# Image statistics of three images: ScalarE sums and squares in place of VectorE's statistics instructions

## The chip, the core and the metric

The kernel runs on one core of a Trainium2 chip. The engines of that core that matter here are TensorE (PE in the profile), VectorE (DVE), ScalarE (ACT), GpSimd (POOL, which issues the gathers) and SyncE (SP, which issues most other DMAs). Each engine works through its own queue in order; what one engine needs from another it waits for at a semaphore. The metric is the device time of one execution in microseconds. It was 2958.33 us before the change, the median of 10 runs (2955.92 to 2961.35).

## The reference

The input is x, four images of 256 channels by 64 x 64 pixels. Cut to what matters, the reference is:

```
x = x + deformable_conv(group_norm(x))     # 3x3, offsets and mask from a 3x3 conv
t = tokens(x)
t = t + attention(layer_norm(t))           # tied over rows, 4 x 4 maps per head
t = t + moe(layer_norm(t))                 # 8 experts, top 2
out = images(t)

group_norm(v): 32 groups of 8 channels; m, s = mean and variance over (8, 64, 64)
               (v - m) / sqrt(s + 1e-5)
```

The change is in the mean and the variance of the group norm. The kernel first makes the mean and the variance of every channel over its 4096 pixels. A small matmul with a block matrix of 1/8 then averages over the 8 channels of a group.

## The kernel before

The convolution comes first. An image is kept as two chunks of 128 channels (ch 0 and 1), 4096 pixels each, in a tile xraw. Its normalised form is turned to pixel rows and stored as a table in device memory. The convolution of an image then takes 288 steps: 32 rows of 128 pixels by 9 taps. The loop of line 1006 runs over the 4 x 288 steps of all images. One step n puts these into the queues, in this order:

- ScalarE: corner0(n + 4), line 808, the first of the four bilinear corners: gathered row times weight into a tile s. It needs the gather of step n + 4.
- VectorE: corners(n + 2), line 817, three multiply-adds (partial, s of the step before, s). The partial needs corner0(n + 2).
- TensorE: turned(n), line 831, two transposes of s into one of three tps tiles.
- ScalarE: to_sbuf(n - 1), line 839, copies a tps tile to sT.
- TensorE: product(n - 5), line 851, one matmul of 128 x 512 into acc.
- whatever else is due at this step, from the list todo.
- POOL: again(n + 1), line 798, the gather of step n + 11 into the buffer that corners has just left. There are ten gather buffers.

The order of VectorE, ScalarE, TensorE and GpSimd in this loop is the order in which it is written (line 997). Everything else for the next image is cut into small pieces that `pieces(b)` (line 438) lays down with a step each, counted from the start of the image that is being convolved. For images 1 to 3 these are: the four loads of 1 MB at steps 8, 18, 28, 38 (LOADS); the statistics of a quarter chunk, one block of 512 pixels a step, from seven steps after each load, so at steps 15 to 18, 25 to 28, 35 to 38 and 45 to 48; then the group means, the deviations and the reciprocal root (a power on GpSimd, line 482); then eight blocks of 512 pixels, 25 steps apart, each normalised on ScalarE (xs, line 549), turned, stored to the table and used for the offsets (po, line 583; oc, line 595; pt, line 604; om, line 615). The offsets become positions and weights on VectorE (lines 650 to 710). The first image makes its own statistics before the loop starts. Four of its own blocks (OWN, line 55) run inside its first steps, from steps 0, 19, 38 and 205.

The group of small PSUM tiles pm, po and pt comes from the pool ps_om, which has two buffers. Behind each block of 36 steps VectorE adds the residual (line 862, at steps 3 and 5 of the following block, so at steps 39 and 41 of an image for its first block), TensorE turns the sum back and ScalarE copies four tiles of it out (line 886, at steps 46, 48, 50, 52 for the first block).

The attention and the experts follow the convolution and are not touched.

The statistics are two lines:

```
V.bn_stats(st[:, ch, j, :], xr[:, ch, j * BLK : (j + 1) * BLK])
if j == NBLK - 1: V.bn_aggr(mv[:, ch, :], ...)
```

Of the kernel before, what the change touches and what calls it, by code (L numbers as in the profile page):

```python
# [9 lines left out]
F32 = mybir.dt.float32  # L10
I32 = mybir.dt.int32
AF = mybir.ActivationFunctionType
ALU = mybir.AluOpType
AX = mybir.AxisListType
# [3 lines left out]
P = 128  # L18
B, C, H, W = 4, 256, 64, 64
HW = H * W  # L20
NCH = C // P
# [16 lines left out]
BLK = 512  # L38
# [19 lines left out]
NBLK = HW // BLK  # L58
# [46 lines left out]
def conv_attn_moe_kernel(  # L105
# [23 lines left out]
    V, S, T, G = nc.vector, nc.scalar, nc.tensor, nc.gpsimd  # L129
# [205 lines left out]
    with ExitStack() as actx:  # L335
        aw = actx.enter_context(tc.tile_pool(name="a_w", bufs=1))
        ag = actx.enter_context(tc.tile_pool(name="a_gather", bufs=1))
        asm = actx.enter_context(tc.tile_pool(name="a_sm", bufs=5))
# [14 lines left out]
        ps_om = actx.enter_context(tc.tile_pool(name="ps_om", bufs=2, space=PSUM))  # L353
# [84 lines left out]
        def pieces(b):  # L438
# [3 lines left out]
            xr = xraw[b]  # L442
            st = asm.tile([P, NCH, NBLK, V.BN_STATS_DIM], F32, name=f"gst{b}", tag="gst", bufs=1)
            mv = asm.tile([P, NCH, V.BN_AGGR_DIM], F32, name=f"gmv{b}", tag="gmv", bufs=2)
# [4 lines left out]
            rs = asm.tile([P, NCH], F32, name=f"rs{b}", tag="grs", bufs=2)  # L449
            pm = []  # L450

            def stats(ch, j):
                V.bn_stats(st[:, ch, j, :], xr[:, ch, j * BLK : (j + 1) * BLK])
                if j == NBLK - 1:
                    V.bn_aggr(mv[:, ch, :], st[:, ch].rearrange("p j s -> p (j s)"))

            def group_of(src):
                pm.append(ps_om.tile([P, NCH], F32, name=f"pm{b}_{len(pm)}", tag="om"))
                T.matmul(pm[-1], group_mean, src, start=True, stop=True)
# [10 lines left out]
            n = FIRST  # L470
            out_ = later if b else first
            for ch in range(NCH):
                for j in range(NBLK):
                    at = LOADS[2 * ch + 2 * j // NBLK] + LANDED + j % (NBLK // 2)
                    out_.append((at if b else n, lambda ch=ch, j=j: stats(ch, j)))
                    n += 1
            out_.append((n + 1, lambda: group_of(mv[:, :, 0])))
            out_.append((n + 2, deviations))
            out_.append((n + 3, lambda: group_of(dv)))
# [262 lines left out]
            for q in range(NBLK + 1):  # L742
                at = n + 10 * q
# [7 lines left out]
            for q in range(EARLY):  # L751
                at = n + 20 * q
# [21 lines left out]
        ss, tps, sTs, accs, sums, backs, outs, last_corner, gathers = ({} for _ in range(9))  # L774
# [219 lines left out]
        for when, fn in pieces(0):  # L994
            todo.setdefault(when, []).append(fn)
        order = {nc.vector.engine, nc.scalar.engine, nc.tensor.engine, nc.gpsimd.engine}
        with tc.manual_schedule(engines=order):
# [8 lines left out]
            for n in range(total + TAP + OUT + 3 * NT):  # L1006
                b, at = divmod(n, STEPS)
                if at == LOADS[0] and b + 1 < B:
                    image_tile(b + 1)
                    for i, when in enumerate(LOADS):  # L1010
                        put_off(b * STEPS + when, lambda b=b, i=i: load_later(b, i))
                    for when, fn in pieces(b + 1):
                        put_off(b * STEPS + when, fn)
                if n < total and n % (NT * K2) == 0:
                    ended(n // (NT * K2))
                if n + LEAD < total:
                    corner0(n + LEAD)
                if n + 1 < total:
                    corners(n + 2)
                if n < total:  # L1020
                    turned(n)
                if LAG <= n < total + LAG:
                    to_sbuf(n - LAG)
                if 0 <= n - TAP < total:
                    product(n - TAP)
                if n == (B - 1) * STEPS + EARLIEST:
                    first_blocks()
                for fn in todo.pop(n, ()):
                    fn()

                if n + 1 + NGB < total:
                    again(n + 1)
# [10 lines left out]
    for b in range(B):  # L1043
        for j in range(NBLK):
            if j < HB:
                n = j * B + b
# [251 lines left out]
    with ExitStack() as bctx:  # L1298
# [266 lines left out]
        chores, sums = [], []  # L1565
# [623 lines left out]
```

## Time and profile before

| what | value |
|---|---|
| median of 10 runs | 2958.33 us (2955.92 to 2961.35) |
| the profiled execution | 2956.37 us, span 2954.7 us |
| busy in the span: PE, DVE, ACT, POOL | 95%, 83%, 64%, 60% |
| statistics, line 453 | 64 instructions, median 684 ns, first at 6.0 us, last at 1000.2 us |
| corners, line 817 | 3 x 1152 instructions, first at 66.5 us, last at 1760 us |
| corner0, line 808 | 1152 instructions, 509 ns each |
| mean granted TensorE clock | 0.992 |

The span runs from the first to the last instruction of one profiled execution. Busy times count an engine's instructions, not its waits. A row of a timeline gives the start, the duration, the engine, the line, the operation and the tiles as out<-in; in brackets stands the idle time before it and what ended it. The duration of a row is longer than its pitch, the time to the start of the next row on the same engine, because an instruction's end overlaps with the next one's start. The pitch is what an instruction costs a full queue.

### The profile page before, as it was taken

How to read it: one execution, taken by the hardware profiler on the slowest of the kernel's cores; microseconds unless marked ns; L12 is line 12 of the kernel's file. 1: busy time of each engine (PE TensorE's matmuls, PEld its weight loads, DVE VectorE, ACT ScalarE, POOL GpSimd, SP SyncE). 2: the span in 40 equal slices, each digit the busy share in tenths (PEclk: the TensorE clock that was granted, in tenths of full speed). 3: DMA queues.
4: the chain of work that ended last, by engine and by line, in shares of the span. 5: the costliest groups of instructions: out<-in, count | busy, mean ns of one | idle time of the engine just before them, and what ended most of it. 6: DMA issues, size and time to landing. Idle time of an engine off the chain costs nothing. (4 is left out here: it accounts for less than half of the span.)

```text
span 2954.7 us, 46107 instructions
## 1 busy us (share of the span) xinstructions
PE 2806.5 (95%) x11358; PEld 1651.6 (56%) x11358; DVE 2460.7 (83%) x6417; ACT 1890.7 (64%) x4459; POOL 1769.7 (60%) x1810
## 2 busy tenths in 40 slices
PE   5899999899998899998999999999999999999997
PEld 3455554455554455543444444445555688888885
DVE  5999989999999999999999987987778685446776
ACT  2666666566765566665766655765875666666675
POOL 2566666666666666667676753321767677774442
PEclk9999999999999999999999999999999999999998
DMA  8999999999999999999999978952565556657988
GB/s 290 368 357 409 406 366 405 405 395 399 406 410 408 380 403 406 403 387 399 399 396 374 387 289 154 170 89 79 184 195 181 176 176 192 205 147 254 339 279 278
DMA packets 347246, 911.97 MB, mean 309 GB/s; under 512 B 42301, under 2 KB 124516, under 8 KB 344679
## 3 DMA queue, kind: packets, MB, share of 16 engines
q0 software_dynamic: 208368, 689.10, 62.7%
q1 hardware_dynamic: 128183, 196.86, 21.4%
q10 hardware_dynamic: 10432, 23.07, 2.0%
q8 instruction: 95, 1.56, 0.2%
q14 instruction: 168, 1.38, 0.1%
HBM read 741.09 MB, written 170.54 MB: 309 GB/s over the span
## 5 line engine op out<-in xcount | busy, mean ns | idle before, releaser
L784 POOL DMA_INDIRECT g<-table,idx x1152 | 1122.0, 974 | 593.4 <-DVE s L817 491.7
L851 PE MATMUL acc<-sT,wconv_sb 128*128 128x512 f32 x2304 | 1183.0, 596 | 18.1 <-ACT sT L839 16.4
L808 ACT ACTIVATE s<-g,wts 128x256 f32<-128x256 f32 x1152 | 586.6, 509 | 327.6 <-DMA g<-table,idx 224.7
L817 DVE SCALAR_TENSOR_TENSOR partial<-g,wts,s 128x256 f32<-128x256 f32 x1152 | 565.0, 490 | 97.1 <-ACT s L808 18.2
L831 PEld LDWEIGHTS tps<-ident,s 128*128 128x128 f32 x2304 | 295.4, 147 | 624.7 <-issue 253.6
L817 DVE SCALAR_TENSOR_TENSOR s<-g,wts,s 128x256 f32<-128x256 f32 x1152 | 550.5, 478 | 0.0
L817 DVE SCALAR_TENSOR_TENSOR s<-g,wts,partial 128x256 f32<-128x256 f32 x1152 | 545.7, 474 | 0.5
L839 ACT COPY sT<-tps 128x256 f32<-128x256 f32 x1152 | 415.6, 361 | 165.0 <-PE acc L851 104.0
L831 PE MATMUL tps<-ident,s 128*128 128x128 f32 x2304 | 456.6, 280 | 61.1 <-DVE s L817 28.8
L1971 POOL DMA_INDIRECT ys_rows<-y,to x277 | 275.9, 996 | 223.0 <-DVE y L1966 166.0
L851 PEld LDWEIGHTS acc<-sT,wconv_sb 128*128 128x128 f32 x2304 | 348.4, 191 | 28.7 <-ACT sT L839 26.1
L1544 POOL DMA_INDIRECT xs_rows<-u,slots x256 | 253.2, 989 | 94.9 <-issue 68.9
L1943 PE MATMUL ph<-xT,w 128*128 128x256 f32 (+1 forms) x1288 | 270.1, 353 | 7.1 <-ACT hT L1947 4.1
L1961 PE MATMUL py<-w,hT 128*128 128x256 f32 x1108 | 266.4, 380 | 0.6 <-ACT w L1910 0.6
L1966 DVE TENSOR_TENSOR y<-py,w 128x512 f32<-128x512 f32 (+1 forms) x161 | 99.3, 617 | 188.9 <-ACT w L1904 81.5
L1943 PEld LDWEIGHTS ph<-xT,w 128*128 128x128 f32 x1288 | 211.9, 191 | 28.3 <-ACT hT L1947 6.1
L1961 PEld LDWEIGHTS py<-w,hT 128*128 128x128 f32 x1108 | 207.2, 190 | 27.4 <-ACT w L1910 1.0
L1947 ACT ACTIVATE hT<-ph,w 128x256 f32<-128x256 f32 (+1 forms) x322 | 136.2, 442 | 130.1 <-PE ph L1943 128.7
L324 DVE SCALAR_TENSOR_TENSOR junk<-q,k 128x512 f32<-128x512 f32 x224 | 141.3, 685 | 19.0 <-ACT k L1143 18.9
L583 PE MATMUL po<-xs,woff_sb 128*96 128x512 f32 x288 | 147.1, 592 | 0.0
L1326 DVE SCALAR_TENSOR_TENSOR mix<-pv,att,mix 128x512 f32<-128x512 f32 x192 | 132.7, 742 | 6.8 <-PE pv L1062 2.8
L1910 ACT COPY w<-early_state 128x768 f32 x161 | 132.8, 825 | 0.0
(294 smaller groups left out, 3436.1 us busy)
## 6 DMA issues: line engine op xcount, KB each, us to landing
xt<-xs_rows SPq DMA_DIRECT2D x116, 260.0 KB
yk<-ys_rows SPq DMA_DIRECT2D x56, 512.0 KB
table<-zt SPq DMA_DIRECT2D x96, 256.0 KB
g<-table,idx POOLq DMA_INDIRECT x1152
t<-o SPq DMA_DIRECT2D x32, 530.0 KB
t<-bo_sb POOLq DMA_DIRECT2D x32, 530.0 KB
dt<-t SPq DMA_DIRECT2D x64, 265.0 KB
xraw<-in_x SPq DMA_DIRECT2D x16, 1024.0 KB
```

What stands on the lines that cost most here:

```text
L324: V.scalar_tensor_tensor(junk, qks[s_, j, ch][0], 1.0, qks[t_, j, ch][1], ALU.mult, ALU.mult, accum_out=parts[:, ch, s_ * B + t_, j : j + 1],)
L583: T.matmul(t["po"], woff_sb[:, ch, ki].rearrange("p kj o -> p (kj o)"), t["xs"][:, ch, ki : ki + RB], start=(n == 0), stop=(n == NCH * 3 - 1),
L784: g = G.indirect_dma_start(out=gs[n % NGB], out_offset=None, in_=tables[b], in_offset=bass.IndirectOffsetOnAxis(ap=params[b][0][:, r, k : ...
L808: first = S.activation(ss[n], gs[n % NGB][:, :C], AF.Copy, scale=params[b][1][:, 0, r, k : k + 1])
L817: last_corner[n] = V.scalar_tensor_tensor(kept if c == 1 else ss[n], gs[n % NGB][:, c * C : (c + 1) * C], params[b][1][:, c, r, k : k + 1] ...
L831: T.transpose(tps[n][:, ch * P : (ch + 1) * P], s[:, ch * P : (ch + 1) * P], ident)
L839: S.copy(sTs[tap][:, :, i * P : (i + 1) * P], tps.pop(n).rearrange("p (ch t) -> p ch t", ch=NCH),)
L851: T.matmul(accs[block, oh], wconv_sb[:, ch, k, oh * P : (oh + 1) * P], sTs[tap][:, ch, :], start=(k == 0 and ch == 0), stop=(k == K2 - 1 a ...
L1544: s = G.indirect_dma_start(out=rows_, out_offset=bass.IndirectOffsetOnAxis(ap=slots[:, k, n : n + 1], axis=0), in_=u[:, n % NT, :], in_off ...
L1943: T.matmul(ph, w1_sb[:, ch, f * P : (f + 1) * P], xT[:, ch, :], start=(ch == 0), stop=(ch == NCH - 1),)
L1961: T.matmul(py[:, i, :], hT[:, f, i * P : (i + 1) * P], w2_sb[:, f, :], start=(f == 0), stop=(f == NCH - 1),)
L1971: s = G.indirect_dma_start(out=ys_rows[g], out_offset=bass.IndirectOffsetOnAxis(ap=to[:, i : i + 1], axis=0), in_=y[:, i, :], in_offset=No ...
```

## The change

For images 1 to 3, `sums` takes the place of `stats`. VectorE still makes the statistics of block 0 of each chunk, and from them an estimate of each channel's mean, of which it keeps the negative (less). ScalarE then goes over each of the eight blocks of a chunk twice: once with Identity and once with Square, both with less as bias, and each with an accumulated sum per channel (powers). The elementwise results go to a junk tile from the pool ps_om. After all sixteen blocks `moments`, five small VectorE operations, makes the mean and the variance from the sums of differences and squares. Everything after that is laid down three steps later than before. The first image keeps its statistics.

```
+            less = asm.tile([P, NCH], F32, ..., tag="less", bufs=1)
+            powers = asm.tile([P, 2, NCH, NBLK], F32, ..., tag="powers", bufs=1)
+
+            def sums(ch, j):
+                part = xr[:, ch, j * BLK : (j + 1) * BLK]
+                if j == 0:
+                    V.bn_stats(st[:, ch, 0, :], part)
+                    V.bn_aggr(mv[:, ch, :], st[:, ch, 0, :])
+                    V.tensor_scalar(
+                        less[:, ch : ch + 1], mv[:, ch, 0:1], -1.0, None, ALU.mult
+                    )
+                junk = ps_om.tile([P, BLK], F32, name=f"junk{b}_{ch}_{j}", tag="om")
+                for k, func in enumerate((AF.Identity, AF.Square)):
+                    S.activation(
+                        junk, part, func, bias=less[:, ch : ch + 1],
+                        accum_out=powers[:, k, ch, j : j + 1],
+                    )
+
+            def moments():
+                both = asm.tile([P, 2, NCH], F32, ..., tag="both", bufs=1)
+                V.tensor_reduce(both, powers, AX.X, ALU.add)
+                V.tensor_scalar(both, both, 1.0 / (H * W), None, ALU.mult)
+                V.tensor_tensor(mv[:, :, 0], both[:, 0], less, ALU.subtract)
+                V.tensor_tensor(both[:, 0], both[:, 0], both[:, 0], ALU.mult)
+                V.tensor_tensor(mv[:, :, 1], both[:, 1], both[:, 0], ALU.subtract)
...
-                    out_.append((at if b else n, lambda ch=ch, j=j: stats(ch, j)))
+                    out_.append((at if b else n, lambda ch=ch, j=j: (sums if b else stats)(ch, j)))
                     n += 1
+            if b:
+                out_.append((n + 2, moments))
+                n += 3
```

More of the change, by code (lines that the diff above doesn't have):

```diff
@@ L450, in pieces @@
             pm = []
+            less = asm.tile([P, NCH], F32, name=f"less{b}", tag="less", bufs=1)
+            powers = asm.tile([P, 2, NCH, NBLK], F32, name=f"powers{b}", tag="powers", bufs=1)
+            def sums(ch, j):
[13 more added lines that the diff above has]
+            def moments():
+                both = asm.tile([P, 2, NCH], F32, name=f"both{b}", tag="both", bufs=1)
+                V.tensor_reduce(both, powers, AX.X, ALU.add)
[3 more added lines that the diff above has]
+                V.tensor_tensor(mv[:, :, 1], both[:, 1], both[:, 0], ALU.subtract)
             def stats(ch, j):
```

## The prediction

> **What bounds the kernel now.** I read the busy slices first, then windows of 10 us around the statistics, then VectorE's waits there, then the timelines of VectorE and ScalarE, row by row. The changed code runs three times, each time in steps 15 to 51 of the image before its own, so only the convolution matters, about 66 to 1760 us. In the busy slices that stage has VectorE and the DMA engines full and ScalarE at six tenths:
>
> ```profile
> DVE  5999989999999999999999987987778685446776
> ACT  2666666566765566665766655765875666666675
> DMA  8999999999999999999999978952565556657988
> ```
>
> Windows of the second image (its 288 steps start at 503 us; columns are length, busy PE, PEld, DVE, ACT, POOL, clock, DMA share, GB/s):
>
> ```profile
> 540.00:550.00 10.00, 8.03 (x26) 3.02 (x24) 9.78 (x24) 5.37 (x15) 5.10 (x7) 1.00 1.02 411
> 560.00:570.00 10.00, 7.51 (x24) 2.73 (x23) 9.91 (x23) 4.43 (x13) 5.82 (x7) 1.00 1.02 413
> 580.00:590.00 10.00, 9.71 (x44) 4.93 (x43) 9.57 (x27) 6.90 (x20) 6.20 (x7) 1.00 1.00 382
> 610.00:620.00 10.00, 10.00 (x36) 4.65 (x35) 9.82 (x28) 6.56 (x17) 6.75 (x8) 1.00 0.96 344
> ```
>
> Two things are full in the stretch of the statistics (up to 582 us): VectorE, and the DMA, at the 411 to 413 GB/s that no window exceeds. Only after it does the DMA fall, to 344, while VectorE stays full. The waits of VectorE from 500 to 660 us are one line:
>
> ```profile
> DVE partial L817 <- ACT s L808: 0.4, 1, 0.4
> ```
>
> VectorE thus sets the pace there, 0.4 us of waiting in 160 us. Its timeline gives the price of one statistics instruction:
>
> ```profile
> 561.62 0.47 DVE L817 SCALAR_TENSOR_TENSOR partial<-g,wts,s 128x256 f32<-128x256 f32 x1
> 562.79 0.68 DVE L453 BATCH_NORM_STATS2 gst<-xraw 128x6 f32<-128x512 f32 x1
> 563.39 0.47 DVE L817 SCALAR_TENSOR_TENSOR partial<-g,wts,s 128x256 f32<-128x256 f32 x1
> ...
> 571.43 0.49 DVE L817 SCALAR_TENSOR_TENSOR partial<-g,wts,s 128x256 f32<-128x256 f32 x1
> 572.79 0.49 DVE L817 SCALAR_TENSOR_TENSOR partial<-g,wts,s 128x256 f32<-128x256 f32 x1
> ```
>
> From one partial to the next is 1.36 us without statistics and 1.77 with: 0.42 us for an instruction 0.68 long, since it covers a bubble. And ScalarE, with the nearest relatives of the new operations:
>
> ```profile
> 559.55 0.51 ACT L808 ACTIVATE s<-g,wts 128x256 f32<-128x256 f32 x1 [0.50 <-DMA g<-table,idx]
> 559.96 0.35 ACT L839 COPY sT<-tps 128x256 f32<-128x256 f32 x1
> ...
> 1386.26 0.51 ACT L273 ACTIVATE l_sq<-bt 128x256 f32<-128x256 f32 x1
> 1386.67 0.19 ACT L273 ACTIVATION_READ_ACCUMULATOR l_sq<-bt 128x1 f32 x1
> 1386.88 0.51 ACT L808 ACTIVATE s<-g,wts 128x256 f32<-128x256 f32 x1
> ```
>
> A step costs ScalarE 0.41 (line 808) + 0.25 (line 839, from its start to a follower's) = 0.66 us. The first row here is corner0 of step 39 of the image (rows of line 808 and partial rows of line 817 counted off in pairs), and the partial at 561.62 is the same step's: VectorE runs 2.07 us behind ScalarE. Call this lag L. It is what VectorE can live on when ScalarE is held up. At steps 29 and 49 it is 4.2 and 7.1 us in the first image, 1.7 and 1.95 in the second, 2.0 and 2.6 in the third. It never falls below 0.54, where VectorE waits.
>
> **The change, part by part.** VectorE, per image: before, 16 statistics at 0.42 and two aggregates. An aggregate makes its step 2.18 and the next 1.29 in place of 1.78 and 1.36: 0.33 each. After: two calls with j = 0, each 0.42 + 0.33 + 0.2 (a third small operation, 0.2 from start to start in the rows of lines 462 to 465) = 0.95. Then five small operations of moments: the four of deviations made their step 1.85 in place of 1.36, 0.49; with one more 0.7 (ends 0.5, the four alone, and 1.0, five at 0.2 with no bubble covered). VectorE alone: 7.4 before, 2.6 after, 4.8 us less an image.
>
> ScalarE, per image: 16 calls of an Identity and a Square of 512 elements, each with an accumulator read: 64 instructions in four bursts of four steps (15 to 18, 25 to 28, 35 to 38, 45 to 48). The square of 256 takes 0.41 to its read, the read 0.21. Another 256 elements add 0.19 (line 297, 597 ns for 256 elements, against line 308, 783 ns for 512). So 0.81 an operation. From below 0.57 + 0.21 (line 595, 504 elements out of PSUM, 0.57 to its follower); from above 0.77 + 0.21 (line 549, 576 elements). A pair is 1.56 to 1.96; I take 1.7, near the square's 1.62, with a little for the Square that waits for the Identity on the same junk tile. Three images: 82 us more on ScalarE.
>
> What of it shows: in a burst a step of ScalarE is 0.66 + 1.7 = 2.36 us against VectorE's 1.36. Queued behind the sums are corner0 of four steps on, for which VectorE waits, and the copy of the turned tile, for which TensorE waits.
>
> Bursts 1 and 3 add a wait: the Identity needs less, made at the end of VectorE's step 15. ScalarE has then done corner0 up to step 19 and VectorE its corners up to 17, so whatever L was, VectorE has two steps left. From that moment corner0 of 20, 21, 22, 23 is done at 2.11, 4.47, 6.83, 9.19; VectorE, at 1.36 from the last start, wants them at 2.72, 4.08, 5.83, 8.19. It stands 0.39 + 1.0 + 1.0 = 2.4 us. Such a burst costs 0.95 + 2.4 - 1.7 (four statistics gone) = +1.65.
>
> Bursts 2 and 4 wait for nothing. ScalarE has the corner0 after the burst done 4 x 2.36 + 0.41 = 9.85 us after its start; VectorE wants it at L + 4 x 1.36. It stands 4.4 - L, or nothing, and saves 1.7. In burst 4 two copies of line 886 (0.28 each) stand in the way as well, and it saves 2.0 with an aggregate.
>
> Second image: burst 1 +1.65. Burst 2: L is 1.7 + 1.65, it stands 1.05: +1.0 in all. Burst 3: +2.65. Burst 4: L is 1.95 + 2.65, it stands 0.3: +0.95. Moments: **+1.65 us**. Third image: VectorE has idle time at steps 24 and 34 (2.64 and 1.71 in place of 1.36), which swallows 1.3 and 0.35; the same steps give **+1.05**. First image: ScalarE also has three oc (0.57) and two xs (0.82) in steps 18 to 20 and again 37 to 39. VectorE stands 0.57 + 0.69 + 0.69 longer after bursts 1 and 3, less 0.86 for two residual sums (0.43 each) that lengthen it in burst 3; bursts 2 and 4 are covered by L of 4 and more. 3.6 - 1.7 + 2.75 - 2.0 + 0.7 = **+3.35**.
>
> Sum: +6.05 us. Ends by the price of a pair: at 1.56 the four steps shrink by 0.14 each, about 0.55 for six coupled bursts: +2.5. At 1.96 they grow by 0.26 each, 1.0 for six coupled and most of four free bursts: +16. The time lost stays lost: behind the stretch VectorE is full to step 96 and the DMA, short of gathers, drops; after that it is at 410 again.
>
> [...]
>
> Costed at nothing. Moments comes three steps later, and with it the blocks of the next image: the last table store moves from about step 251 to 254; the first gather of that image is issued at about 277, more than 20 steps on. Without that cover it would cost 3 x 1.4 = 4.3 us an image. On SP a t1 store changes places with four table stores; on POOL the pow (0.73 us) falls three gathers later; both queues have spare time (POOL is busy 5 to 6 of 10 us). The junk tiles share the two om buffers with po, pt and pm: in the first image po holds one, the junk the other; the next user, pt, comes 3 steps after a burst. If ScalarE is later than that, TensorE waits, 1 to 2 us twice. Identity, Square and Copy need no more table loads than before: the loads in the instruction order are the same six.
>
> The profiled execution took 2956.4 us (span 2954.7); 2956.4 + 6.0 = 2962.4. It stands 2.0 under the median of 2958.3, so the forecast is **2964.4 us**.
>
> **Rivals.** (1) *ScalarE's bursts hide and VectorE's relief counts: faster.* For it: ScalarE is idle for half of each window. Its size is capped: until step 49 gathers come at the full DMA rate, so VectorE can gain no more than L - 0.54 there: 6.6, 1.4 and 2.0 us, of which the first is held to 4.8. Sum -8.2: 2950. It decides if a pair costs under about 1.2 us. Against it: a pair has two reads at 0.21 alone. (2) *Relief and stalls cancel*: VectorE's idle time and the ten gather buffers take up the stalls as in the third image: +1, 2959. For it: the DMA is as full as VectorE, so some lateness costs nothing. (3) *Worse*: pairs at 1.96 or more, and TensorE held up through the copies and the om buffers, 1 to 2 us for each of six coupled bursts: 16 + 9 = +25, 2983. Against it: TensorE is busy 7.5 to 8 of 10 us there and can catch up.
>
> **How the numbers follow.** My forecast 0.60 (+2.5 to +16, its own range 2961 to 2974), rival 1 0.17, rival 2 0.10, rival 3 0.13. The least that this kernel's measurement tells from no change is 0.2%, 5.9 us. The forecast's case straddles it, 0.36 above and 0.24 below. Slower 0.36 + 0.13, same 0.24 + 0.10, faster 0.17. The range 2952 to 2979 cuts off the lower half of rival 1 and the upper part of rival 3.
>
> **What would show it.** Right: in steps 15 to 24 and 35 to 44 VectorE waits on ScalarE's line 808 (now in 0.4 us of 160), 2 to 4 us a burst; Identity and Square rows of 0.6 to 0.8 us with reads of 0.19; 14 statistics fewer an image and a pitch of 1.36 in steps 26 to 29 that breaks once. Wrong: no such waits with VectorE free after step 49 (rival 1), or idle time on TensorE behind ScalarE's copies (rival 3). The least certain is the pair's price; 0.1 us of it is 2 to 4 us.

## The result: 0.48% slower, and the profile after

The changed kernel took 2972.0 us (median of 8 runs, 2967.51 to 2976.35) where the kernel before took 2958.3 us beside it (28 runs, 2954.45 to 2962.27). The ratio is 1.0048, with a 95% interval of 1.0039 to 1.0057. The forecast was 2964.4 us; the loss is 13.7 us in place of 6. Its own trace has a span of 2970.2 us, 15.5 us above that of before.

The busy slices of the profile after, each digit the busy tenths of one fortieth of the span:

```profile
DVE  5889989899999899999999996888778685446777
ACT  2766665766665766665776665765875666666675
DMA  8989999999999999999999978952555556647988
```

VectorE loses a tenth in the second and third slices, the DMA one in the third, and ScalarE gains one in the second. That is the first image, whose steps carry the statistics of the second. Counting the partials step by step in both traces (their starts at the same step of the same image) gives the loss by place:

| stretch | before | after | difference |
|---|---|---|---|
| up to the first step of the loop | 66.5 us | 67.8 us | +1.3 |
| first image, steps 12 to 60 | 79.3 | 91.4 | +12.1 |
| first image, steps 60 to 288 | 335.2 | 333.3 | -1.9 |
| second image, steps 12 to 60 | 74.1 | 75.8 | +1.7 |
| third image, steps 12 to 60 | 75.7 | 77.1 | +1.4 |
| fourth image, all steps | 412.9 | 411.8 | -1.1 |
| behind the convolution | 1195.9 | 1197.5 | +1.6 |

So one stretch of 80 us holds nearly the whole loss. The first and the last row hold nothing that the change touches; in a second trace of the changed kernel (below) they are +0.1 and +0.5, so 2 to 3 us of the 15.5 are not the change's. VectorE's waits from 88 to 185 us are these; before the change it had one, and that behind step 60 (at 175 us), none within the stretch:

```profile
DVE om L615 <- PE pt L604: 0.8, 1, 0.8
```

And after:

```profile
DVE partial L846 <- ACT s L837: 11.4, 11, 2.6
DVE om L644 <- PE pt L633: 5.4, 2, 3.5
DVE gm L488 <- PE pm L485: 0.9, 1, 0.9
DVE both L472 <- ACT junk L465: 0.8, 1, 0.8
```

VectorE now stands 18.5 us there. 11.4 of it is for corner0, behind ScalarE's sums; 5.4 is for pt, a small TensorE matmul; the last two are for the group means and for the moments. ScalarE's timeline of the third burst shows the queue (start, duration, operation, idle time before it):

```profile
136.90 0.69 ACT L465 ACTIVATE junk<-xraw,less 128x512 f32<-128x512 f32 x1 [1.97 <-DVE less L460]
137.53 0.18 ACT L465 ACTIVATION_READ_ACCUMULATOR junk<-xraw,less 128x1 f32 x1
...
138.47 0.49 ACT L837 ACTIVATE s<-g,wts 128x256 f32<-128x256 f32 x1
...
140.69 0.49 ACT L837 ACTIVATE s<-g,wts 128x256 f32<-128x256 f32 x1
...
143.47 0.49 ACT L837 ACTIVATE s<-g,wts 128x256 f32<-128x256 f32 x1
...
144.24 0.68 ACT L624 ACTIVATE oc<-po,boff_sb 32x512 f32<-32x512 f32 x1
144.94 0.92 ACT L578 ACTIVATE xs__1165<-xraw,nb,rs 128x640 f32<-128x640 f32 x1
...
147.31 0.49 ACT L837 ACTIVATE s<-g,wts 128x256 f32<-128x256 f32 x1
```

A pair (the Identity, the Square, which is not shown, and their two reads) takes 138.47 - 136.90 = 1.57 us, and corner0 comes every 2.22 us (138.47, 140.69), then after 2.78 and 3.84 where the image's own oc and xs stand in the queue as well. VectorE, behind it, at the same time:

```profile
141.22 0.49 DVE L846 SCALAR_TENSOR_TENSOR partial<-g,wts,s 128x256 f32<-128x256 f32 x1 [0.48 <-ACT s L837]
144.00 0.49 DVE L846 SCALAR_TENSOR_TENSOR partial<-g,wts,s 128x256 f32<-128x256 f32 x1 [0.90 <-ACT s L837]
147.84 0.49 DVE L846 SCALAR_TENSOR_TENSOR partial<-g,wts,s 128x256 f32<-128x256 f32 x1 [2.57 <-ACT s L837]
150.26 0.49 DVE L846 SCALAR_TENSOR_TENSOR partial<-g,wts,s 128x256 f32<-128x256 f32 x1 [0.56 <-ACT s L837]
156.36 0.27 DVE L644 COPY om<-pt 128x108 f32<-128x108 f32 x1 [3.46 <-PE pt L633]
```

The last row has no sum anywhere near it: the burst's last corner0 was done 8 us earlier. It is TensorE that is late. Its timeline:

```profile
144.27 0.44 PE L860 MATMUL tps<-ident,s 128*128 128x128 f32 x2 [1.48 <-ACT sT L868]
144.55 1.02 PE L880 MATMUL acc<-sT,wconv_sb 128*128 128x512 f32 x2
148.25 0.69 PE L860 MATMUL tps<-ident,s 128*128 128x128 f32 x2 [2.69 <-ACT sT L868]
150.68 2.08 PE L880 MATMUL acc<-sT,wconv_sb 128*128 128x512 f32 x2 [1.74 <-ACT sT L868]
152.55 0.89 PE L633 MATMUL pt<-tap_sum,oc 96*128 96x27 f32 x4
153.26 0.67 PE L860 MATMUL tps<-ident,s 128*128 128x128 f32 x2
153.72 1.91 PE L880 MATMUL acc<-sT,wconv_sb 128*128 128x512 f32 x2
155.43 0.89 PE L633 MATMUL pt<-tap_sum,oc 96*128 96x27 f32 x4
```

TensorE waits for ScalarE's copies three times, then has the delayed transposes and products to do in order before the pt matmuls at 152.55 and 155.43. The products take 2.08 and 1.91 us where they took 1.02 just before. Windows of 4 us for TensorE alone (length, busy, count, granted clock, DMA share, GB/s) show the clock:

```profile
104.00:108.00 4.00, 2.62 (x9) 1.00 1.02 418
108.00:112.00 4.00, 1.17 (x3) 0.71 1.02 406
112.00:116.00 4.00, 4.00 (x11) 0.50 1.01 401
116.00:120.00 4.00, 4.00 (x18) 0.94 0.83 279
...
144.00:148.00 4.00, 1.30 (x4) 0.90 1.01 408
148.00:152.00 4.00, 2.01 (x4) 0.50 0.63 219
152.00:156.00 4.00, 4.00 (x13) 0.50 0.76 244
156.00:160.00 4.00, 4.00 (x13) 0.82 0.33 85
```

In and behind the windows in which TensorE works only 1.2 to 1.3 us of 4, its granted clock falls to 0.50; by the windows it stands at half for 6.8 and for 10.2 us. In the trace of before it is 1.00 in the same windows. So little work does not always bring it down: in the second trace of this kernel it stays at 1.00 through the first burst (below). The last column is the other trace of the stall: gathers are issued when VectorE frees a buffer (of the 607.5 us that GpSimd stands idle ahead of its gathers in the trace after, 502.3 end with VectorE's s), and the DMA falls to 85 GB/s. TensorE's longest stops in the two bursts were 2.00 us (before the product at 111.27 us) and 2.69 us (above). What sets the clock back is not shown.

### The profile page after: what moved, and what is told of

Its sections match the earlier page's. It is cut to its first block, busy times and chain, and to the rows that moved or that the text cites. A ratio compares the mean times of both kernels' runs of the same rounds, so it can differ in the third digit from the quotient of the medians.

```text
span 2970.2 us, 46243 instructions
## 1 busy us (share of the span) xinstructions
PE 2811.6 (95%) x11358; PEld 1661.1 (56%) x11358; DVE 2442.0 (82%) x6396; ACT 1956.1 (66%) x4651; POOL 1770.0 (60%) x1810
## 3 DMA queue, kind: packets, MB, share of 16 engines
q8 instruction: 95, 1.56, 0.2%
## 5 line engine op out<-in xcount | busy, mean ns | idle before, releaser
L813 POOL DMA_INDIRECT g<-table,idx x1152 | 1121.8, 974 | 607.5 <-DVE s L846 502.3
```

What stands on the lines that cost most here:

```text
L813: g = G.indirect_dma_start(out=gs[n % NGB], out_offset=None, in_=tables[b], in_offset=bass.IndirectOffsetOnAxis(ap=params[b][0][:, r, k : ...
```

## The experiments

Four explanations were weighed for the 12 us: the queue of ScalarE, made longer by the image's own oc and xs; the wait of the sums for less; the two om buffers that the junk tiles share with po and pt; and TensorE's clock. The first eight runs, in two groups, were on a slower chip, on which the kernel before took 3350.2 us beside the first four and 3303.3 us beside the next four. Ratios hold against those. The changed kernel itself did not run there, so the totals of the runs with sums in all three images have nothing to stand beside. Stretches are compared among those runs alone, and only for steps 12 to 60 of the first image, where the DMA reached 407 and 414 GB/s there too (windows at 104 and 140 us; 412 and 405 before). Even in this stretch every run on that chip, with sums or without, has a wait for corner0 of 1.2 to 2.9 us at steps 16 to 18, ahead of the first sum in ScalarE's queue, which no trace of the other chips has. Differences of less than some 2 us between these stretches therefore say nothing.

**The first image's steps without sums, the others as after.** VectorE's statistics stay for the second image.

```
-  ... (sums if b else stats)(ch, j)
+  ... (sums if b > 1 else stats)(ch, j)
-            if b:
+            if b > 1:
                 out_.append((n + 2, moments))
```

> The sums on ScalarE for the third and fourth image alone; the second image's statistics, which fall into the steps of the first image, stay on VectorE. Theory A (the loss sits in the first image, where the bursts meet ScalarE's own oc and xs of that image and TensorE idles so long that its clock falls to half): by the two traces 10 us of the 14 are lost in the first image, 2.1 in the second, 1.4 in the third; so +3.5 us, 2961.8. Rival B (the extra work on ScalarE costs the same wherever it stands): two thirds of 13.7, +9.1, 2967.4.

Ratio 1.0058 (1.0039 to 1.0076), 3367.85 us. The first image's stretch was 80.8 us. The same kernel again:

> The sums on ScalarE for the third and fourth image alone, a second time, since on the chip of the first time the kernel before took 3350 us and kept its gathers back at some 350 GB/s. Theory A (10 of the 14 us are lost in the first image, where the bursts meet ScalarE's own oc and xs and TensorE's clock falls to half): +3.5 us where the kernel before takes 2958. Rival B (the cost follows the work on ScalarE alone): +9 us.

Ratio 1.0041 (1.0023 to 1.0060), 3313.84 us; the stretch 81.8 us. These two stretches, with VectorE's statistics in them, are the base for the other runs on this chip, since no trace of the kernel before was taken there.

**Only the first image's steps with sums.**

```
-  ... (sums if b else stats)(ch, j)
+  ... (sums if b == 1 else stats)(ch, j)
-            if b:
+            if b == 1:
                 out_.append((n + 2, moments))
```

> The sums on ScalarE for the second image alone, the one whose bursts fall into the first image's steps. Theory A: +10 us, 2968.3, with TensorE's granted clock at half in two stretches near 112 and 150 us. Rival B: a third of 13.7, +4.6, 2962.9.

Ratio 1.0021 (1.0006 to 1.0037), 3357.32 us. The stretch took 93.2 us, 11 to 12 more than the base, as on the first chip. VectorE's waits from 88 to 185 us are nearly those of after: 11.3 us for corner0, 4.4 for pt.

Here the two groups cannot be read by their totals: the 12 us are there in the stretch, but only 7 us of them at the end, and the kernel without them loses more, 10 to 18 us. Behind step 60 the traces of that chip differ by more than is sought: the kernel of the two runs above took 381.9 and 365.4 us for steps 60 to 288 of the first image. What the last two images cost on that chip is left open.

**The bursts moved off oc and xs.** The statistics of the second image go to steps 21, 28, 42 and 48, between the oc and xs of the first image's own blocks.

```
                     at = LOADS[2 * ch + 2 * j // NBLK] + LANDED + j % (NBLK // 2)
+                    if b == 1:
+                        at = (21, 28, 42, 48)[2 * ch + 2 * j // NBLK] + j % (NBLK // 2)
...
             if b:
+                n += 2 if b == 1 else 0
                 out_.append((n + 2, moments))
```

> The changed kernel with the second image's four bursts moved off the steps in which ScalarE makes oc and xs for the first image: to steps 21, 28, 42 and 48 in place of 15, 25, 35 and 45, with everything behind them two steps later. Theory A: the first image then loses 2 to 4 us like the others and TensorE's clock stays at full in its steps 12 to 60; 2958.3 + 3 + 3.5 = 2965. Rival B: no change against the changed kernel, 2972.

Ratio 1.0119 (1.0094 to 1.0143), 3387.37 us. The stretch took 88.9 us: 4.3 less than the run above, and still 7 to 8 above the base. Without the early wait at steps 16 to 18 (2.9 us here, 1.5 in the run above) it is 5.7 less. So moving the bursts away from oc and xs takes away a third to a half of the loss, and a burst without them still costs. VectorE's waits from 88 to 185 us, against 11.4 and 5.4 after:

```profile
DVE partial L849 <- ACT s L840: 5.9, 6, 2.9
DVE partial L849 <- ACT junk L465: 3.1, 3, 1.3
DVE both L472 <- ACT junk L465: 3.0, 1, 3.0
DVE om L647 <- PE pt L636: 1.6, 1, 1.6
```

Waits of 5.9 + 3.1 us behind ScalarE are left, 2.9 of them the early wait, and the later last burst now holds up moments for 3.0. Since the new places bring waits of their own, the price of oc and xs alone is not separated.

**No sums at all.** Block 0's statistics stand for the chunk.

```
-                junk = ps_om.tile([P, BLK], F32, ...)
-                for k, func in enumerate((AF.Identity, AF.Square)):
-                    S.activation(junk, part, func, bias=..., accum_out=...)
...
             if b:
-                out_.append((n + 2, moments))
                 n += 3
```

> The changed kernel with no sums and no moments at all: the statistics of the first 512 pixels of each chunk stand for the chunk (the mean and variance over the other 3584 pixels are left out), and everything behind stays three steps later. It gives the most that relief of VectorE can bring. The prediction's cap (VectorE gains no more than its lag behind ScalarE, since gathers come at the full DMA rate): 4.6 + 1.4 + 2.0 us, 2950. Without the cap: 14 statistics at 0.42 less and 0.3 to 0.9 more an image, three times 5 to 6, 2941 to 2943. If the three steps' delay is what costs: 2958 or more.

Ratio 1.0005 (0.9981 to 1.0029), 3349.56 us; the stretch 77.7 us. The same kernel again:

> No sums and no moments, the first 512 pixels' statistics standing for the chunk, everything behind three steps later; a second time for the same reason. The prediction's cap: -8 us. Without the cap: -15 to -18 us. If the three steps' delay costs: 0 or more.

Ratio 1.0014 (0.9998 to 1.0029), 3307.11 us; the stretch 76.9 us. In that stretch VectorE's relief is worth 3.1 to 4.9 us against the base, near the 4.8 that the prediction set as the cap of a gain there. VectorE then waits for TensorE in it, 1.8 us twice in the first run. At the end the gain is gone, behind step 60, where that chip's traces are too far apart to say why. Whether it would be kept on the first chip was not measured.

**No wait for less.** The sums are taken about zero, so that VectorE's three instructions before a chunk go, and with them the wait.

```
+        nought = aw.tile([P, NCH], F32, name="nought")
+        G.memset(nought, 0.0)
...
-                if j == 0:
-                    V.bn_stats(st[:, ch, 0, :], part)
-                    V.bn_aggr(mv[:, ch, :], st[:, ch, 0, :])
-                    V.tensor_scalar(less[:, ch : ch + 1], mv[:, ch, 0:1], -1.0, None, ALU.mult)
...
-                        junk, part, func, bias=less[:, ch : ch + 1],
+                        junk, part, func, bias=nought[:, ch : ch + 1],
```

> The changed kernel with a constant 0 subtracted in place of the estimate less: VectorE makes no statistics at all for these images and ScalarE never waits for it; bursts, moments and places stay. In the second and third image bursts 1 and 3 then stand 4.1 - L like the others: by the prediction's own sums +1 us each, no better than the 1.7 and 1.1 of the changed kernel. In the first image ScalarE starts bursts 1 and 3 some 2 us sooner. If that wait is what sets off the loss there (theory A1): 4 to 6 us in place of 10, 2966. If the burst itself suffices (A2): 2970 to 2972.

Ratio 1.0111 (1.0082 to 1.0140), 3337.50 us. The stretch took 93.6 us, with 12.0 us of waits for corner0 and 5.6 for pt. The stretch is no shorter than with the wait for less (93.2 us in the run with sums in the first image only), so that wait is not the cause. Either way ScalarE's lead is used up within the burst: VectorE's corners run 0.5 us behind corner0 at step 24 in both kernels, and 2.8 before.

**One operation a step.** From step 17 to 44 an Identity or a Square a step, then eight between 45 and 50; the same work, without bursts.

```
+                when = [*range(17, 33), *range(37, 45), 45, 46, 47, 47, 48, 49, 49, 50]
+                for m, at in enumerate(when):
+                    ch, j, k = m // (2 * NBLK), m // 2 % NBLK, m % 2
+                    out_.append((at, lambda ch=ch, j=j, k=k: one_sum(ch, j, k)))
```

> The same sums, one ScalarE operation a step in place of two a step in bursts (steps 17 to 32, 37 to 50; the last eight in six steps), estimates at steps 15 and 35 as before, moments and everything behind two steps later than in the changed kernel. A step of ScalarE is then 0.66 + 0.79 = 1.45 us against VectorE's 1.36. Theory A: no stall of more than 1 us, TensorE does not idle and keeps its clock; the first image loses 0 to 3 us, the others gain 0 to 2: 2956 to 2962. Rival B: 2972, the work is the same.

Ratio 1.0017 (1.0002 to 1.0032), 3309.09 us. The stretch took 82.8 us: 1.0 to 2.0 above the base, no more than these stretches can tell, where bursts cost 11 to 12. It is the burst that costs most, not the 16 x 1.57 = 25 us of ScalarE's work. Waits of 6.1 us for corner0 (1.9 of them the early one) and 2.3 for pt are left.

The next three were on a chip like the first; the kernel before took 2959.63 us there. **The changed kernel again:**

> The changed kernel as it is, beside the next two. It gives the change's price on a chip on which the gathers may be slow, and a second profile of the first image's steps 12 to 60, which took 79.3 us before and 91.4 after in the first pair of profiles. Expected there: 90 to 94 us, with TensorE's clock at half in two stretches. Over all: +0.48% on a chip like the first; on the slow one the sum of its two parts there, 0.2 + 0.5 = 0.7%.

Ratio 1.0037 (1.0023 to 1.0051), 2969.81 us. Stretches of 90.1, 76.9 and 77.4 us: the loss and its place repeat. One thing does not. In the first burst the clock stays at 1.00 (windows of TensorE as above), the product behind it takes 1.13 us and not 2.08, and of the two waits for pt only that behind the third burst is left:

```profile
104.00:108.00 4.00, 1.71 (x7) 1.00 1.01 407
108.00:112.00 4.00, 2.00 (x8) 1.00 1.03 411
```

```profile
110.13 1.13 PE L880 MATMUL acc<-sT,wconv_sb 128*128 128x512 f32 x2 [2.00 <-ACT sT L868]
```

```profile
DVE om L644 <- PE pt L633: 3.5, 1, 3.5
```

The copy for which this product waits is as late as in the first trace (2.00 us in both). So the same backlog makes VectorE wait 1.96 us at half clock and not at all at full clock.

**The junk tiles out of the om buffers**, in a buffer of their own in SBUF.

```
-                junk = ps_om.tile([P, BLK], F32, name=f"junk{b}_{ch}_{j}", tag="om")
+                junk = atmp.tile([P, BLK], F32, name=f"junk{b}_{ch}_{j}", tag="junk", bufs=1)
```

> The changed kernel with the junk tile in SBUF instead of one of the two small PSUM buffers that po, pt and pm use. If TensorE waits for that buffer (the prediction's 1 to 2 us twice): steps 12 to 60 of the first image 2 to 4 us shorter than in the changed kernel. [...]

Ratio 1.0035 (1.0021 to 1.0049), 2969.18 us; the first stretch 90.4 us, between the changed kernel's 90.1 and 91.4, waits 11.0 and 4.8. The shared buffers play no part that shows. The clock falls here twice, to 0.50 at 108 and 144 us.

**TensorE kept busy.** The same, junk in SBUF, with one more matmul of 128x512 (two rows in the trace) ahead of the transposes in steps 15 to 21 and 35 to 42 of the first image, whose result nobody reads.

```
+                if n in (*range(15, 22), *range(35, 43)):
+                    warm = ps_om.tile([P, BLK], F32, name=f"warm{n}", tag="om")
+                    T.matmul(warm, ident, wconv_sb[:, 0, :2]..., start=True, stop=True)
```

> The same with the junk in SBUF, and one idle matmul of 128x512 (its result is read by nobody) in front of turned in steps 15 to 21 and 35 to 42 of the first image, so that TensorE has 0.86 us more to do in each and does not fall idle behind ScalarE's copies. Theory C (part of the first image's loss is TensorE at half clock after its idle time: the 3.5 us in which VectorE waits for pt, and matmul pairs of 2 us in place of 1): the clock stays at 0.9 or more and steps 12 to 60 take 84 to 87 us. Rival D (the loss is ScalarE's queue alone, the clock falls but nothing waits for it): 90 us or more, and more than in the run with the junk in SBUF alone.

Ratio 1.0029 (1.0017 to 1.0042), 2967.34 us. The clock now holds through the first burst, and is at half for less time behind the third, by the windows 3.4 us where the run above has 10.2:

```profile
108.00:112.00 4.00, 4.00 (x14) 1.00 1.02 408
...
144.00:148.00 4.00, 2.50 (x9) 1.00 0.83 311
148.00:152.00 4.00, 3.76 (x11) 0.71 0.74 208
```

```profile
149.56 1.96 PE L1051 MATMUL warm<-wconv_sb,ident 128*128 128x512 f32 x2
```

The wait for pt behind the first burst falls from 1.36 us in the run above to 0.56; behind the third it stays at 3.4. The stretch takes 89.3 us, 1.1 less than the run above and 0.8 to 2.1 less than the changed kernel, whose own two traces differ by 1.3. That is less than theory C had (84 to 87 us), but it is not the whole price of the clock: the added matmuls stand in TensorE's queue themselves. The last row is one of them, at half clock, ahead of the late pt; the next row starts 1.75 us later.

For the third burst of the changed kernel the price can be estimated from rows. From the product at 150.68 us to the end of the pt at 155.43 TensorE took 5.6 us. With the pitches that the same operations have at full clock in the second trace (0.96, 0.40, 0.27, 0.87 and 0.53 us, between 110 and 114.3 us) it would be 3.0. So of the 3.46 us of waiting about 2.6 are the clock, and with the 1.96 behind the first burst some 4.6 of the 5.4. The wait for pt thus takes both, a backlog in an ordered queue and a clock at half. What the clock takes of the 12 us lies between the 1 to 2 us measured and this estimate, and is not settled.

**VectorE's statistics for the second image, spread sums for the third and fourth.** The edit of "one operation a step", with `if b > 1:` in place of `if b:`.

> VectorE's statistics stay for the image whose statistics run beside the first image's steps (its burst cost about 12 us there); for the last two images ScalarE makes the sums, one operation a step from step 17 to 50 in place of bursts of eight in four steps. The computation is the whole of it. Theory (the bursts cost, since ScalarE's queue goes ahead of VectorE's by only two steps and TensorE's by one; the work itself has room on ScalarE): steps 12 to 60 of the first image as before (79.3 us), of the second and third 72 to 76 us each (before 74.1 and 75.7, the changed kernel 75.8 and 77.1), VectorE's waits for corner0 there under 2 us an image; 2955 to 2959 us where the kernel before takes 2958 to 2960, a ratio of 0.9985 to 1.000. Rival (82 us of work on ScalarE costs wherever it stands, or moments, three steps later, costs by itself): the second and third stretch stay 1.4 to 1.7 us longer than before, 2961 to 2963 us, a ratio of 1.001 or more. On a chip whose gathers come at 350 GB/s neither could show, as VectorE waits for gathers there: 1.000 within 0.0015.

2962.03 us beside 2959.46, ratio 1.0007 (0.9998 to 1.0016). The first stretch is back at 79.4 us, as before the change (79.3), on a chip like the first. The second and third took 74.4 and 75.0 us, as the theory had it (74.1 and 75.7 before), but steps 60 to 288 behind them took 328.9 and 333.7 in place of 326.7 and 331.9, and the waits for corner0 were 5.5 and 6.2 us, not under 2. So nothing is gained, and whether 0.1% is lost is not settled by the interval. (The trace is of the slowest of the eleven executions. Of its 9.9 us more than before, 1.5 stand ahead of the loop and 6.2 behind the convolution, where nothing was changed; the convolution itself is 2.2 longer.) Two rows show where relief goes. ScalarE, then VectorE, in this run:

```profile
542.03 0.51 ACT L845 ACTIVATE s<-g,wts 128x256 f32<-128x256 f32 x1 [1.73 <-DMA g<-table,idx]
```

```profile
542.57 0.49 DVE L854 SCALAR_TENSOR_TENSOR partial<-g,wts,s 128x256 f32<-128x256 f32 x1 [0.69 <-ACT s L845]
```

Freed of statistics, VectorE catches up with ScalarE, and ScalarE with the gathers; the DMA stands at 413 GB/s from 540 to 550 us, where it had 411 before. Four such waits, at steps 26, 27, 33 and 34, make 3.1 of the 5.5 us. Another 2.1, at steps 52 to 54, have no gather in them: there ScalarE is full itself, busy 9.97 us of the 10 from 580 to 590, since the last eight sums stand in six steps beside the copies of the block's result. Spreading the sums further was not tried. This version beats the changed kernel by 8 to 10 us and not the kernel before.

## Why the forecast was right in its sign and short in its size

**The mechanism held.** ScalarE feeds VectorE and is full in a burst (busy 3.94 us of the 4 from 104 to 108 us); VectorE waits for corner0 there. In the second image's first burst the partials came at these steps in the timeline after:

```profile
543.60 0.49 DVE L846 SCALAR_TENSOR_TENSOR partial<-g,wts,s 128x256 f32<-128x256 f32 x1
...
545.57 0.49 DVE L846 SCALAR_TENSOR_TENSOR partial<-g,wts,s 128x256 f32<-128x256 f32 x1 [0.70 <-ACT s L837]
...
547.79 0.49 DVE L846 SCALAR_TENSOR_TENSOR partial<-g,wts,s 128x256 f32<-128x256 f32 x1 [0.95 <-ACT s L837]
...
550.01 0.49 DVE L846 SCALAR_TENSOR_TENSOR partial<-g,wts,s 128x256 f32<-128x256 f32 x1 [0.95 <-ACT s L837]
```

Steps of 1.97, 2.22 and 2.22 in place of 1.36 are 0.61 + 0.86 + 0.86 = 2.3 us; the working said 2.4. The step with less was 2.20 long, 0.84 more, where 0.95 was said.

**The price of a pair** was taken at 1.7 us, between 1.56 and 1.96. It is 1.57, at the lower end.

**Second and third image**: forecast +1.65 and +1.05, measured +1.7 and +1.4 in their stretches (+2.8 and +1.7 in the repeat). Right, and for its reason: in the second image the working has 2.4 + 1.05 + 2.4 + 0.3 = 6.15 us of waits for corner0, and the trace has 6.4.

**First image**: forecast +3.35, measured +12.1, and 10.8 in the repeat. This is the term of the sum that was mis-sized. Its parts, from the timeline after:
- Waits for corner0 of bursts 1 and 3: said 2.4 + 1.95 = 4.35 and 4.35 - 0.86 = 3.49. Measured 0.43 + 0.95 + 1.50 + 1.02 + 1.17 = 5.07 and 0.48 + 0.90 + 2.57 + 0.56 = 4.51. Together 1.7 too little.
- Bursts 2 and 4, "covered by L of 4 and more": 0.95 and 0.84 us of waits, 1.8 too little. L was 3.8 in place of 7.1 at step 49. Burst 2 came late itself: the row below shows ScalarE's copy, just ahead of its first sum, held up by TensorE's backlog, and so the loss goes round in a circle.

```profile
119.94 0.37 ACT L868 COPY sT<-tps 128x256 f32<-128x256 f32 x1 [2.49 <-PE acc L880]
```

- The wait for pt: costed at nothing in the sum. The sentence "If ScalarE is later than that, TensorE waits, 1 to 2 us twice" named the place, but tied it to the om buffers and left it out; rival 3 was put aside since "TensorE is busy 7.5 to 8 of 10 us there and can catch up". It measured 1.96 + 3.46 = 5.4 us, 3.5 in the repeat and 4.8 without the om buffers. This is the step that failed: the backlog of three delayed copies stands in order ahead of pt, and the clock halves on top. At a clock of 1.00, behind the first burst of the repeat, TensorE did catch up as rival 3's answer had it; at 0.50 it did not.
- The group means and the moments waited 0.9 and 0.8 us for TensorE and ScalarE, which the working did not have.

These come to 10.7 us of waits more than said; the stretch came to 8.8 more than said. The rest is VectorE's own work: it waited 18.5 us and lost 12.1, so its work in the stretch is 6.4 us less, where the working took off 4.5.

**The range.** The working gave +2.5 us for a pair at 1.56 us and +16 for one at 1.96. The pair came out at 1.57, so by the working's own rule the loss should have been near the lower end. That 13.7 lies within the range is luck: the upper end stood there for a dearer pair, and what reached it was TensorE's backlog and clock, and longer waits for corner0, in the first image.

**"The time lost stays lost"** is true to 1.9 us, which came back in the first image behind step 60, in both traces.

**Rivals.** Rival 1, that VectorE's relief counts, fell: the waits are there. Its cap of 4.8 us for the first stretch fits the 3.1 to 4.9 us of the run without sums. Rival 3 had the right place, TensorE held up through the copies, but the om buffers had no part in it that shows, pairs cost 1.57 and not 1.96, and it struck in two bursts of one image and not in six.

## What to carry to other kernels

Work moved to an engine with idle time cost here by where it stood in that engine's queue: ScalarE ran ahead of VectorE by a few steps only, so a burst longer than that lead stalled VectorE (11.4 us of waits for corner0 in the first image), and through TensorE's ordered queue it also delayed pt, which has nothing to do with the burst (5.4 us of waits, with the clock at 0.50). Price a burst against the lead at that point and follow each delayed result to its second consumer (here copy, transposes, pt); one operation a step took most of the loss away (a stretch 1.0 to 2.0 us above the base, where bursts cost 11 to 12). Relief of the fullest engine went as far as the next full resource, here gathers at 413 GB/s and then ScalarE itself, busy 9.97 us of 10.

## What was unexpected in the hardware

TensorE's clock fell to 0.50 inside the convolution, in windows in which the trace of before has 1.00. TensorE's longest stop around it was 2.69 us, and products of 1.02 us then took up to 2.08. The same kernel's second trace, with nearly the same stops in the first burst, kept it at 1.00 there.

And one chip was slower. The kernel before took 344 to 392 us longer there, 12 to 13%. In the trace of the run with sums in the first image only, the convolution is 207 us longer than in that of before and what follows it 194. The gathers look slower: by fortieths of the span the DMA stands at 330 to 389 GB/s from the second to the twenty-second, where the changed kernel on the first chip has 377 to 411 from the fourth. But ScalarE hardly waits for them, against what was expected of the last run above. Rows of the page of before, then of that run (busy us, mean ns, then the idle time before and what ended most of it):

```profile
L808 ACT ACTIVATE s<-g,wts 128x256 f32<-128x256 f32 x1152 | 586.6, 509 | 327.6 <-DMA g<-table,idx 224.7
L839 ACT COPY sT<-tps 128x256 f32<-128x256 f32 x1152 | 415.6, 361 | 165.0 <-PE acc L851 104.0
```

```profile
L837 ACT ACTIVATE s<-g,wts 128x256 f32<-128x256 f32 x1152 | 590.3, 513 | 62.7 <-DMA g<-table,idx 24.3
L868 ACT COPY sT<-tps 128x256 f32<-128x256 f32 x1152 | 424.1, 368 | 543.2 <-PE tps L860 197.5
```

Waits for gathers fall from 224.7 to 24.3 us, and the copies of the turned tiles wait 543 us in place of 165. By these rows slow gathers are not what holds the convolution up there; what does, no run here shows.
